# A 1024-by-256 matrix product inside a graph-network kernel, done with seven smaller products instead of eight

## The chip, the cores and the metric

The kernel runs on one core of a Trainium2 chip. The metric is the time of one execution on the device, in microseconds. The kernel before takes 3191.79 us, the median of three runs that lie between 3191.39 and 3193.04. The profile is of one more execution, whose span is 3188.7 us.

## What is computed

There are 64 graphs of 256 nodes with 256 features, and an integer adjacency matrix for each. Two layers follow one another. The first is two rounds of graph attention, then a norm, a feed-forward with ReLU, and a norm. The second is an attention with eight heads in which the adjacency value chooses which of several value matrices a pair of nodes uses, and then again a norm, a feed-forward with GELU, and a norm. Cut to the part that is changed:

```python
B, N, F = x.shape            # 64, 256, 256
# ... layer 0: two graph attentions, layernorm, relu feed-forward, layernorm
# ... layer 1: q, k, v, masked attention over 8 heads, output projection
x = _ln(src + attn_out, g1, beta1)
ff = jax.nn.gelu(x @ W1 + b1, approximate=False) @ W2 + b2     # W1: 256x1024, W2: 1024x256
return _ln(x + ff, g2, beta2)
```

Everything is in 32-bit floats. "The second product of the second feed-forward" is the multiplication by `W2`.

## The kernel before

Two graphs make a unit, so that there are 32 units of 512 rows. The program is a row of turns. In one turn three units are at work: `y_` in its second layer (attention, then the GELU feed-forward), `x_` in the ReLU feed-forward, and `z` in its two graph attentions. The order of TensorE and of the SyncE queue is that of the program text. VectorE (DVE), ScalarE (ACT) and GpSimd (POOL) are ordered by a scheduler; `behind(...)` keeps it from issuing an operation ahead of a marked one. There are six PSUM banks for general use (`bank`), besides one for `po` and one for `zo`.

```python
def turn(y_, x_, z):
    q, k_ = queries_keys(y_, hT)
    scores(0)                       # exponentials of the first quad of heads
    v = values(y_, hT, range(T))
    scores(1); piece(); sums(0)
    first_hidden(range(0, 2)); scores(2); sums(1)
    first_hidden(range(2, 5)); scores(3); piece()
    first_hidden(range(5, 8))
    # ... early(z), load_x(z + 1)
    sums(2); sums(3)
    out_(0); piece(); project(z); out_(1); first_rows(z)
    normed(y_, 2, y)
    # ... transposes of y_ by DVE and small DMAs; first_softmax(z); affine passes
    hidden_out(x_, 0, X["y"], X["h1"], wf2)
    for n, _ in enumerate(hidden_seven(y_, 1, hT, w1s, b1, AF.Gelu, h1)):
        if Z and n > 1:
            Z["hp"] = gat_first(z, Z["s"], Z["xp"], Z.get("hp"), range(2 * n - 4, 2 * n - 2))
    with behind("copied"):
        normed(x_, 1, X["y"])
    # ... transposes of x_, affine
    second_scores(z)                # rows by TensorE, then the softmax
    if waiting:
        finish(*waiting.pop(), 0, G)    # last norm of the unit of the turn before
    # ... (the last two turns differ)
    for t in range(T):
        if t == T - 1:
            second_sums(z)
        hidden_out_block(y_, 1, y, h1, w2, t)
    waiting.append((y_, y))
```

The first product of the GELU feed-forward already uses seven products for a two-by-two split (`hidden_seven`). The second product is done block by block, each of 128 rows, with 256 moving columns:

```python
def hidden_out_block(u, l, y, h1, wo_, t):
    b, i = divmod(t, NB)
    if i == 0:
        hidden_ps[u, l] = bank(f"yfp{l}_{u}_{b}")
    ps = hidden_ps[u, l]
    for k in range(FB):             # 8 blocks of the 1024 hidden features
        nc.tensor.matmul(ps[:, i * F:(i + 1) * F], h1[:, k, t * P:(t + 1) * P], wo_[:, k, :],
                         start=(k == 0), stop=(k == FB - 1))
    if i == NB - 1:
        yb = y[:, b * NB:(b + 1) * NB, :].rearrange("p t f -> p (t f)")
        nc.vector.tensor_tensor(yb, ps, yb, ALU.add)
```

The division of the attention ends with a check sum on ScalarE, and small vectors are brought in through a shared buffer of the tag `rz`:

```python
def divided(u, b, po, zo, oT):
    rz = work.tile([P, KB * N], F32, tag="rz", name=f"rz{u}_{b}")
    nc.vector.reciprocal(rz, zo)
    nc.vector.tensor_tensor(oT[:, :, b * N:(b + 1) * N], ...)
    nc.scalar.activation(rz, rz, AF.Identity, accum_out=low[:, u * G + b:u * G + b + 1])

def normed(u, l, y, blocks=range(T)):
    for t in blocks:
        nc.vector.bn_stats(...); nc.vector.bn_aggr(...)
    nc.gpsimd.tensor_scalar(rs, ...); nc.gpsimd.tensor_tensor(rs, rs, mhalf, ALU.pow)
    nc.vector.scalar_tensor_tensor(nm, ...)
    for t in blocks:
        nc.scalar.activation(y[:, t, :], y[:, t, :], AF.Identity, bias=nm[:, t:t + 1], scale=rs[:, t:t + 1])
```

Of the kernel before, what the change touches and what calls it, by code (L numbers as in the profile page):

```python
# [16 lines left out]
P = 128  # L17
# [368 lines left out]
def narrow_path(  # L386
# [97 lines left out]
    def columns(vs, name, queue):  # L484

        ns = [v.shape[0] // P for v in vs]
        rows = work.tile([P, KB * N], F32, tag="rz", name=f"{name}r")[:, 0:P]
        t = const.tile([P, sum(ns)], F32, name=name)
        at, views = 0, []
        for v, n in zip(vs, ns):  # L490
            queue.dma_start(rows[at:at + n, :], v.rearrange("(c p) -> c p", p=P))
            views.append(t[:, at:at + n])
            at += n
        ps = bank(f"{name}p")
        nc.tensor.transpose(ps[:, :at], rows[:at, :], ident[:at, :at])
        nc.vector.tensor_copy(t, ps[:, :at])
        return views
# [61 lines left out]
    def seven(w, name):  # L559
# [9 lines left out]
        return a11, a12, a22, s1, s2, a21, s4  # L569


    def shifted(w, blocks, shift, bias, name):
# [11 lines left out]

    w1s = []

    def folding():
# [19 lines left out]
        scaled(w1, lg3)  # L607
        w1s.extend(seven(w1, "w1"))
        yield

# [3 lines left out]
    for rb, v, name in ((rb1, g_bf2, "rbf2"), (rb2, t_bo, "rbo"), (rb3, t_b2, "rbt2")):  # L614
        nc.gpsimd.tensor_add(rb, rb, row(v, name, work.tile([P, KB * N], F32, tag="rz", name=name)[:, :F]))

# [10 lines left out]
    def to_features(src, name):  # L627

        dst = work.tile([P, KB, TN], F32, tag="hT", name=name)
        for k in range(KB):  # L630
            ps = bank(f"{name}p{k}")
            for t in range(T):
                nc.tensor.transpose(ps[:, t * P:(t + 1) * P], src[:, t, k * P:(k + 1) * P], ident)
            nc.vector.tensor_copy(dst[:, k, :], ps)
        return [dst[:, k] for k in range(KB)]
# [7 lines left out]
    def normed_features(u, l, xn, natural=False, queues=(nc.sync,)):  # L643
# [7 lines left out]
        if natural:  # L651
            hT = work.tile([P, KB, TN], F32, tag="hT", name=f"hT{u}_{l}")
            to = hT.rearrange("c k (t a r) -> c (k t) a r", a=Q, r=32)
            for q in range(Q):
                for a in range(Q):
                    nc.sync.dma_start(to[q * 32:(q + 1) * 32, :, a],
                                      yt[a * 32:(a + 1) * 32, q].rearrange("c k t r -> c (k t) r"))
            return [hT[:, k] for k in range(KB)]
# [82 lines left out]
    def add_blocks(u, name, y, b, lhs, rhs, n):  # L741
# [7 lines left out]
        yb = y[:, b * NB:(b + 1) * NB, :].rearrange("p t f -> p (t f)")  # L749
        nc.vector.tensor_tensor(yb, ps, yb, ALU.add)  # L750

# [38 lines left out]
    def hidden_seven(u, l, hT, w, bi, func, h1):  # L790
# [58 lines left out]
        for h in halves:  # L849
            product(two[h], h, s1, moving(0), True)  # L850
            p5[h] = copied(h, 1, two[h])
        for h in halves:
            product(two[h], h, s4, quarter[1][1], False)
            copied(h, 0, two[h])
# [8 lines left out]
        for h in halves:  # L863
            product(one[h], h, s3, moving(2), False)
            added(h, 1, 1, p5[h])
        yield
        for h in halves:
            product(one[h], h, a22, moving(3), False)
            done(h, 1, 0, one[h])
            done(h, 1, 1)  # L870

    def hidden_out_block(u, l, y, h1, wo_, t):
# [7 lines left out]
        if i == NB - 1:  # L880
            yb = y[:, b * NB:(b + 1) * NB, :].rearrange("p t f -> p (t f)")
            nc.vector.tensor_tensor(yb, ps, yb, ALU.add)

    hidden_ps = {}
# [32 lines left out]
    def weighted(u, b, m, q, k_, aT):  # L917
# [13 lines left out]
        for a in range(HPB):  # L931
            nc.scalar.activation(e[:, a, :], ps[a], AF.Exp, scale=isd)  # L932
        for a in range(0, HPB, 2):
            nc.vector.tensor_tensor(ea[:, a:a + 2, :], e[:, a:a + 2, :],  # L934
                                    ab[:, None, :].to_broadcast([P, 2, NB * N]), ALU.mult)
        es = work.tile([P, HPB, N], F32, tag="es", name=f"es{n}")
        nc.vector.tensor_add(es, e[:, :, 0:N], e[:, :, N:2 * N])
        return e, ea, es
# [14 lines left out]
    def divided(u, b, po, zo, oT):  # L953
        rz = work.tile([P, KB * N], F32, tag="rz", name=f"rz{u}_{b}")
        nc.vector.reciprocal(rz, zo)  # L955
        nc.vector.tensor_tensor(oT[:, :, b * N:(b + 1) * N],
                                po.rearrange("p (m n) -> p m n", m=KB),
                                rz.rearrange("p (m n) -> p m n", m=KB), ALU.mult)
        nc.scalar.activation(rz, rz, AF.Identity, accum_out=low[:, u * G + b:u * G + b + 1])

# [22 lines left out]
    def first_scores(z):  # L983
        first_rows(z)
        first_softmax(z)

    def second_scores(z):
        d = g[z]
        d["s"] = gat_softmax(z, 1, d["hp"], score_rows(z, 1, d["hp"], F), F + 1, F, d["aT"])

# [13 lines left out]

    def out_pieces(u, y, h1):

        for t in range(T):
            hidden_out_block(u, 1, y, h1, w2, t)
            b, i = divmod(t, NB)
            if i == NB - 1:  # L1010
                finish(u, y, b, 1)
            yield

    def finish(u, y, b, n):

        bt = slice(b * NB, (b + n) * NB)
        normed(u, 3, y, range(b * NB, (b + n) * NB))
        with behind("added"):
            affine(y[:, bt, :], rg4, rb4)
# [6 lines left out]
    def turn(y_, x_, z):  # L1026
# [11 lines left out]
        def sums(n):  # L1038
# [4 lines left out]
            if m == KB - 1:  # L1043
                divided(y_, b, *acc[b], oT)

        def first_hidden(blocks):
            if X:
                X["h1"] = hidden(x_, 0, X["hT"], wf1, bf1, AF.Relu, blocks, X.get("h1"))

        scores(0)  # L1050
# [7 lines left out]
        first_hidden(range(2, 5))  # L1058
        scores(3)
        piece()  # L1060
        first_hidden(range(5, 8))
        if Z:
            early(z)
        if z + 1 < NG:
            load_x(z + 1)
        sums(2)
        sums(3)

# [15 lines left out]
        if Z:  # L1084
            with behind("transposed", "placed"):
                first_softmax(z)
        if X:
            affine(X["y"], rg1, rb1)
# [11 lines left out]
        if X:  # L1100
            with behind("copied"):
                normed(x_, 1, X["y"])
            X["hT"] = (normed_features(x_, 1, X["y"], natural=True) if Z
                       else to_features(X["y"], f"h2T{x_}"))
            with behind("added"):
                affine(X["y"], rg2, rb2)
        if Z:
# [3 lines left out]
        if Z:  # L1111
            second_scores(z)
        if waiting:
            with behind("scaled" if Z else "copied"):
                finish(*waiting.pop(), 0, G)
        if y_ >= NG - 2:
            last = out_pieces(y_, y, h1)
            if X:
                left.append(last)
            else:  # L1120
                for _ in last:
                    pass
            return
        for t in range(T):
            if t == T - 1:
                second_sums(z)
            hidden_out_block(y_, 1, y, h1, w2, t)
        waiting.append((y_, y))
# [6 lines left out]
    with tc.manual_schedule(engines={mybir.EngineType.PE, mybir.EngineType.SP}):  # L1135
# [20 lines left out]
        normed(0, 1, g[0]["y"])  # L1156
        next(fold)
        second_sums(1)
        g[0]["hT"] = to_features(g[0]["y"], "h2T0")
        affine(g[0]["y"], rg2, rb2)  # L1160
        for u in range(NG):
            turn(u, u + 1, u + 2)
# [54 lines left out]
```

## Time and profile before

| | before |
|---|---|
| time, median of 3 | 3191.79 us |
| span of the profiled execution | 3188.7 us |
| TensorE matmuls busy | 3137.3 us |
| TensorE weight loads busy | 2178.4 us |
| VectorE busy | 2117.7 us |
| ScalarE busy | 1547.8 us |
| GpSimd busy | 412.1 us |
| DMA traffic over the span | 37 GB/s |

The page of a profile gives each engine's busy time, then the span in 40 slices, then the chain of work that ended last, then groups of instructions. The timeline lists an engine's instructions in order: the start in microseconds from the beginning of the span, the time from the first start to the last end, the engine, the line of the kernel, the operation, output and input by name, the shape, and how many like it follow each other. The end of a matmul is modelled and overlaps the start of the next, so that the cost of a group is best read from its start to the start of the next group. A line number may be that of a helper.

### The profile page before, as it was taken

Reading aid. Unit: us, or ns where it says so; the run is one execution under the profiler, and the core shown is the slowest. Engines: PE = TensorE matmul, PEld = TensorE weight load, DVE = VectorE, ACT = ScalarE, POOL = GpSimd, SP = SyncE. Lnnn points to the kernel's source line nnn. Section 1 sums busy time; section 2 is a strip of 40 time slices with the busy share of each in tenths; the row PEclk is TensorE's granted clock in tenths of the full one; section 3 lists DMA queues with packets and bytes.
Section 4 is the critical chain, followed back from the end, with each engine's and each line's share of the span. In section 5 each row is a group of like instructions: output and inputs, shape, how many; then the busy total and the mean of one; then the engine's idle time right before and its main releaser. Section 6 shows DMA issues by size and latency. Waiting matters only on the chain.

```text
span 3188.7 us, 46935 instructions
## 1 busy us (share of the span) xinstructions
PE 3137.3 (98%) x17584; PEld 2178.4 (68%) x17584; DVE 2117.7 (66%) x3870; ACT 1547.8 (49%) x3076; POOL 412.1 (13%) x633
## 2 busy tenths in 40 slices
PE   8899999999999999999999999999999999999997
PEld 5577766677766677666677666777666776667755
DVE  3566666666676666676666666666766666766655
ACT  4255544555544545545545445554445455455543
POOL 1111011011011111110110110110101111101100
PEclk9999999999999999999999999999999999999999
DMA  5011112121111121121211121211112111211000
GB/s 144 19 37 37 21 35 44 39 44 29 26 39 40 42 44 26 24 43 39 44 37 22 34 44 39 44 29 24 40 39 44 40 28 25 44 39 31 24 12 15
DMA packets 461160, 117.09 MB, mean 37 GB/s; under 512 B 397400, under 2 KB 460288, under 8 KB 460928
## 3 DMA queue, kind: packets, MB, share of 16 engines
q1 hardware_dynamic: 450592, 106.60, 15.4%
q10 hardware_dynamic: 9280, 6.39, 0.7%
q8 instruction: 141, 2.31, 0.3%
q0 software_dynamic: 1056, 1.05, 0.1%
q14 instruction: 91, 0.75, 0.1%
HBM read 57.04 MB, written 16.78 MB: 23 GB/s over the span
## 4 chain that ended last, share of the span: by engine, by line
PE 91%; DVE 4%; ACT 1%; POOL 1%; DMA 1%; ACTq 1%; issue 1%; SPq 0%; DVEq 0%; POOLq 0%
PE yfp L878 24%; PE h1p L785 14%; PE po L947 7%; PE vp L910 7%; PE h1a L820 6%; PE sp L926 4%; PE h1b L820 4%; PE qp L897 4%; PE yop L747 4%; PE kp L897 3%; PE hpp L736 3%; PE xpp L694 3%; PE ygp L747 3%; PE zo L950 2%; POOL rs L764 1%; DVE st L761 1%
## 5 line engine op out<-in xcount | busy, mean ns | idle before, releaser
L934 DVE TENSOR_TENSOR ea<-e,aT 128x1024 f32<-128x1024 f32 x256 | 302.2, 1222 | 285.1 <-ACT e L932 285.1
L768 ACT ACTIVATE y<-y,nm,rs 128x256 f32<-128x256 f32 x512 | 269.4, 591 | 420.2 <-DVE nm L765 420.2
L878 PE MATMUL yfp<-w,h 128*128 128x256 f32 x2048 | 452.9, 379 | 0.0
L785 PE MATMUL h1p<-hT,wf 128*128 128x512 f32 x992 | 450.6, 602 | 0.0
L878 PE MATMUL yfp<-wf,h 128*128 128x256 f32 x2048 | 448.5, 380 | 0.0
L878 PEld LDWEIGHTS yfp<-wf,h 128*128 128x128 f32 x2048 | 387.8, 191 | 52.2 <-issue 0.5
L878 PEld LDWEIGHTS yfp<-w,h 128*128 128x128 f32 x2048 | 386.6, 190 | 51.9 <-DVE v L912 0.3
L932 ACT ACTIVATE e<-sp 128x512 f32<-128x512 f32 x512 | 263.7, 603 | 224.4 <-PE sp L926 218.1
L785 PEld LDWEIGHTS h1p<-hT,wf 128*128 128x128 f32 x992 | 180.6, 189 | 228.7 <-issue 193.1
L648 DVE STREAM_TRANSPOSE yt<-y 128x256 f32<-128x256 f32 x368 | 151.7, 431 | 214.7 <-ACT y L768 201.0
L787 ACT ACTIVATE h<-h1p,cols 128x512 f32<-128x512 f32 x256 | 172.8, 692 | 239.0 <-PE h1p L785 239.0
L763 POOL TENSOR_SCALAR rs<-mv 128x4 f32<-128x4 f32 (+1 forms) x130 | 29.1, 232 | 1751.0 <-DVE mv L762 1743.8
L955 DVE RECIPROCAL rz<-zo 128x512 f32<-128x512 f32 x64 | 214.7, 3354 | 53.6 <-PE zo L950 53.6
L665 POOL COPY hT<-yt 32x256 f32<-32x256 f32 x248 | 215.8, 870 | 191.9 <-DVE yt L648 166.1
L775 DVE TENSOR_TENSOR y<-y,rg 128x1024 f32<-128x1024 f32 (+1 forms) x130 | 157.0, 1209 | 98.5 <-ACT y L768 94.2
L910 PE MATMUL vp<-wv,hT 128*128 128x512 f32 x480 | 214.0, 599 | 0.0
L761 DVE BATCH_NORM_STATS2 st<-y 128x6 f32<-128x256 f32 x512 | 195.3, 408 | 4.5
L826 ACT COPY cp<-h1b 128x512 f32<-128x512 f32 x192 | 111.1, 581 | 113.4 <-PE h1b L820 70.1
L910 PEld LDWEIGHTS vp<-wv,hT 128*128 128x128 f32 x480 | 88.7, 190 | 110.4 <-issue 103.2
L776 DVE TENSOR_TENSOR y<-y,rb 128x1024 f32<-128x1024 f32 (+1 forms) x130 | 161.2, 1242 | 3.2
L830 DVE TENSOR_TENSOR h<-h1a,cp 128x512 f32<-128x512 f32 x192 | 130.3, 682 | 45.7 <-PE h1a L820 45.6
L696 ACT COPY xp<-xpp 128x260 f32<-128x260 f32 x128 | 47.6, 373 | 232.6 <-PE xpp L694 232.5
(183 smaller groups left out, 4773.1 us busy)
## 6 DMA issues: line engine op xcount, KB each, us to landing
hT<-yt SPq DMA_DIRECT2D x1038, 32.0 KB, 1.9
y<-in_x_dram SPq DMA_DIRECT2D x32, 512.0 KB, 4.0
xq<-in_x_dram SPq DMA_DIRECT2D x240, 64.0 KB, 2.3
aq<-in_adj_dram SPq DMA_DIRECT2D x240, 64.0 KB, 2.4
out_dram<-y SPq DMA_DIRECT2D x30, 512.0 KB
hT<-yt ACTq DMA_DIRECT2D x186, 32.0 KB, 1.9
wf<-in_L_gnn_w_ff_dram SPq DMA_DIRECT2D x2, 1024.0 KB, 7.1
w<-in_L_gnn_W_dram SPq DMA_DIRECT2D x2, 1024.0 KB
```

Of the source, the lines that this page charges most:

```text
L665: nc.gpsimd.tensor_copy(to, at)
L747: nc.tensor.matmul(ps[:, i * F:(i + 1) * F], lhs(t, k), rhs(b, k), start=(k == 0), stop=(k == n - 1))
L761: nc.vector.bn_stats(st[:, t, :], y[:, t, :])
L768: mark["normed"] = nc.scalar.activation(y[:, t, :], y[:, t, :], AF.Identity, bias=nm[:, t:t + 1], scale=rs[:, t:t + 1])
L785: nc.tensor.matmul(ps, wi[:, k, f * P:(f + 1) * P], hT[k], start=(k == 0), stop=(k == KB - 1))
L820: nc.tensor.matmul(ps[:, i * N:(i + 1) * N], w_[:, f * P:(f + 1) * P], m, start=first and i == 0, stop=True, skip_group_check=True)
L878: nc.tensor.matmul(ps[:, i * F:(i + 1) * F], h1[:, k, t * P:(t + 1) * P], wo_[:, k, :], start=(k == 0), stop=(k == FB - 1))
L897: nc.tensor.matmul(ps, w[:, k, m * P:(m + 1) * P], hT[k], start=(k == 0), stop=(k == KB - 1))
L910: nc.tensor.matmul(ps, hT[k][:, t * P:(t + 1) * P], wvf[:, k, :], start=(k == 0), stop=(k == KB - 1))
L932: nc.scalar.activation(e[:, a, :], ps[a], AF.Exp, scale=isd)
L934: nc.vector.tensor_tensor(ea[:, a:a + 2, :], e[:, a:a + 2, :], ab[:, None, :].to_broadcast([P, 2, NB * N]), ALU.mult)
L947: nc.tensor.matmul(po[hp, m * N:(m + 1) * N], vs[:, hp], w[:, a, j * N:(j + 1) * N], start=(n == 0), stop=(n == len(terms) - 1))
```

## The change

The 512x1024 matrix of hidden values and the 1024x256 weights are each split in two by two. With sums of the quarters taken first, seven products of quarters give the result in place of eight. The sums of the weights are taken once, on GpSimd; those of the hidden values in each turn, on VectorE. The purpose is less work for TensorE. The rest of the change makes room for it: the last norm of a unit is moved into the next turn, behind the exponentials of the third quad; the check sum after a division is moved away from it; a few copies change engine; in the second transposition of `x_` four of sixteen small DMAs become copies on GpSimd; and the last part of the folding of weights at the start comes after the second norm.

```diff
-        rows = work.tile([P, KB * N], F32, tag="rz", name=f"{name}r")[:, 0:P]
+        rows = work.tile([P, KB * N], F32, tag="rz", name=f"{name}r", bufs=1)[:, 0:P]
...
+    def seven_out(w, name):
+        h = F // 2
+        b11, b12, b21, b22 = (w[:, k * FB // 2:(k + 1) * FB // 2, o * h:(o + 1) * h]
+                              for k in range(2) for o in range(2))
+        t1, t2, t4 = (const.tile([P, FB // 2, h], F32, name=f"{name}t{n}") for n in (1, 2, 4))
+        nc.gpsimd.tensor_tensor(t1, b12, b11, ALU.subtract)
+        nc.gpsimd.tensor_tensor(t2, b22, t1, ALU.subtract)
+        nc.gpsimd.tensor_tensor(t4, b21, t2, ALU.subtract)
+        nc.gpsimd.tensor_tensor(b12, b22, b12, ALU.subtract)
+        return b11, b21, b22, t1, t2, b12, t4
...
     def to_features(src, name):
-            nc.vector.tensor_copy(dst[:, k, :], ps)
+            nc.scalar.copy(dst[:, k, :], ps)
...
     def normed_features(..., natural=True):
-                    nc.sync.dma_start(to[q * 32:(q + 1) * 32, :, a], ...)
+                    move = nc.gpsimd.tensor_copy if q == a else nc.sync.dma_start
+                    move(to[q * 32:(q + 1) * 32, :, a], ...)
...
     def hidden_seven(...):
             product(one[h], h, s3, moving(2), False)
             added(h, 1, 1, p5[h])
+            done(h, 1, 1)
         yield
         for h in halves:
             product(one[h], h, a22, moving(3), False)
             done(h, 1, 0, one[h])
-            done(h, 1, 1)
...
+    def hidden_out_seven(u, l, y, h1, w, s1, s2, s3, s4):
+        b11, b21, b22, t1, t2, t3, t4 = w
+        K2, F2 = FB // 2, F // 2
+        a11, a12, a21, a22 = (h1[:, k * K2:(k + 1) * K2, b * N:(b + 1) * N]
+                              for b in range(2) for k in range(2))
+        nc.vector.tensor_tensor(s1, a21, a22, ALU.add)
+        nc.vector.tensor_tensor(s2, s1, a11, ALU.subtract)
+        nc.vector.tensor_tensor(s4, a12, s2, ALU.subtract)
+        mark["quarters"] = nc.vector.tensor_tensor(s3, a11, a21, ALU.subtract)
+
+        def product(ps, a, w_, first):
+            for i in range(NB):
+                for k in range(K2):
+                    nc.tensor.matmul(ps[:, i * F2:(i + 1) * F2], a[:, k, i * P:(i + 1) * P], w_[:, k, :],
+                                     start=first and i == 0 and k == 0, stop=True, ...)
+
+        def added(b, o, ps):
+            yq = y[:, b * NB:(b + 1) * NB, o * F2:(o + 1) * F2]
+            nc.vector.tensor_tensor(yq, ps[:, :F].rearrange("p (i f) -> p i f", i=NB), yq, ALU.add)
+
+        product(one, a11, b11, True);  added(0, 0, one);  yield
+        product(two, s1, t1, True);    added(1, 1, two);  yield
+        product(ps, a12, b21, True);   added(0, 0, ps);   yield
+        product(one, s2, t2, False);   added(0, 1, one);  yield
+        product(two, s4, b22, False);  added(0, 1, two);  yield
+        product(one, s3, t3, False);   added(1, 1, one);  yield
+        product(one, a22, t4, False);  added(1, 0, one);  yield
...
     def divided(u, b, po, zo, oT):
-        rz = work.tile([P, KB * N], F32, tag="rz", name=f"rz{u}_{b}")
+        rz = work.tile([P, KB * N], F32, tag="rz", name=f"rz{u}_{b}", bufs=1)
...
+        return rz
+
+    def noted(u, b, rz):
         nc.scalar.activation(rz, rz, AF.Identity, accum_out=low[:, u * G + b:u * G + b + 1])
...
     def turn(y_, x_, z):
         scores(3)
+        with behind("exp3"):
+            noted(y_, 0, acc[0])
         piece()
...
+        if waiting:
+            finish(*waiting.pop(), 0, G, ("summed1", "exp2"), ("divided0",))
         sums(2)
         sums(3)
...
             with behind("transposed", "placed"):
                 first_softmax(z)
+                noted(y_, 1, acc[1])
...
-            with behind("copied"):
+            with behind("fifth"):
                 normed(x_, 1, X["y"])
...
-            second_scores(z)
-        if waiting:
-            with behind("scaled" if Z else "copied"):
-                finish(*waiting.pop(), 0, G)
+            second_rows(z)
...
-        for t in range(T):
-            if t == T - 1:
+        for n, _ in enumerate(pieces):
+            if Z and n == 2:
+                second_softmax(z)
+            if Z and n == 5:
                 second_sums(z)
-            hidden_out_block(y_, 1, y, h1, w2, t)
...
         normed(0, 1, g[0]["y"])
-        next(fold)
         second_sums(1)
         g[0]["hT"] = to_features(g[0]["y"], "h2T0")
         affine(g[0]["y"], rg2, rb2)
+        next(fold)
```

The seven bodies of the products are put on one line each here, and the names of banks are left out. In the last two turns the seven products are cut at each `yield` into pieces, which fill places among the exponentials.

## The prediction
> **What bounds the kernel now.** I read the busy shares first, then the slices, the chain of waits, and one turn of the steady state in the timeline, engine by engine.
>
> ```profile
> PE 3137.3 (98%) x17584; PEld 2178.4 (68%) x17584; DVE 2117.7 (66%) x3870; ACT 1547.8 (49%) x3076; POOL 412.1 (13%) x633
> ...
> PEclk9999999999999999999999999999999999999999
> ...
> PE 91%; DVE 4%; ACT 1%; POOL 1%; DMA 1%; ACTq 1%; issue 1%; SPq 0%; DVEq 0%; POOLq 0%
> ```
>
> TensorE is busy 98% of the span at full clock and makes up 91% of the chain that ended last; DVE has a third of its time free. The kernel is a row of 32 turns, and one turn in the middle lasts 96.58 us (from the first `h1b` matmul at 1526.02 to the next at 1622.60). Adding up start-to-start times in that turn leaves about 1 us without matmul issue. So only TensorE time, or a new TensorE wait, can move the result by much. The part that is replaced stands in the timeline of TensorE so:
>
> ```profile
> 1541.87 0.60 PE L703 MATMUL rows<-ident,hp 128*128 128x128 f32 x4
> 1542.31 10.53 PE L878 MATMUL yfp<-w,h 128*128 128x256 f32 x48
> 1552.67 3.62 PE L747 MATMUL ygp<-hp,s 128*128 128x256 f32 x16
> 1556.13 3.62 PE L878 MATMUL yfp<-w,h 128*128 128x256 f32 x16
> 1559.58 3.60 PE L897 MATMUL qp<-hT,wq 128*128 128x512 f32 x8
> 1563.01 3.60 PE L897 MATMUL kp<-hT,wk 128*128 128x512 f32 x8
> ```
>
> Columns: start, length, engine, line, form, count. The second product takes 10.36 + 3.45 = 13.81 us of each turn, counted start to start. It has 32 matmuls in the program and 64 records: an f32 matmul appears as two records, each with its own weight load. One record costs 13.81 / 64 = 216 ns at 256 columns; at 512 columns, from `qp`, (1563.01 − 1559.58) / 8 = 429 ns. So a record costs about 3 ns + 0.832 ns per column, and at 128 columns I expect 109.5 ns from the moving side.
>
> [...] The new matmuls stream 128 columns for each load of 128 weight columns, a balance this kernel never had. [...] The start of the trace has the two halves apart:
>
> ```profile
> 22.96 1.04 PE L679 MATMUL aTp<-ident,first 128*128 128x128 f32 x8
> 23.83 1.04 PE L633 MATMUL xT1p<-ident,y 128*128 128x128 f32 x8
> ...
> 53.92 1.84 PE L576 MATMUL b1sp<-cols,w 128*128 128x1 f32 x16
> ```
>
> Eight transposes, each with a load and 128 moving columns, take 23.83 − 22.96 = 0.87 us: 109 ns each, agreeing with the line above. The `b1sp` matmuls move one column per load, so they show the load's pace: (1.84 − 0.25) / 15 = 106 ns[...]. (Their records show loads of 190 ns, but these overlap; a transpose's load is shown with 137 ns, so it is perhaps a lighter one, and the transposes don't prove the balanced case.) No run shows both sides full at once.
>
> **The change part by part.**
>
> *Product.* Out: 64 records × 216 ns = 13.81 us. In: seven products × 2 row blocks × 4 k-blocks = 56 matmuls = 112 records of 128 columns. Columns fall from 8192 to 7168, by an eighth. 112 × 109.5 ns = 12.26 us. Gain **1.55 us a turn**, if loads hide.
>
> *Sums on DVE.* Four sums of quarters of 128x1024 cost 1.22 us each (the `es` row of the same shape), 4.9 us; seven additions of 128x256 at about 0.42 us (as the `tt` subtractions of that size), 2.9 us; two additions of 0.66 us go. Net +6.5 us a turn, so DVE busy goes from 66 us to some 73 of 95 us: not the bound. The order matters: product 1 needs no sum and covers 1.75 us; the second needs the first sum, whose input (the quarter for the second graph's upper half) has its GELU moved forward. Walking the turn with the old durations, that GELU ends near 1541.5, the first sum near 1542.8, and product 2 starts near 1544; the last sum is done near 1546.5, seven to eight us before product 6 ends. `second_sums` needs the scaled `hp` near 1553.3 and gets it near 1552.6. Narrow, but free.
>
> *ScalarE order.* The `rows` transposes wait for the last two `hp` copies. Before, they ran just in time:
>
> ```profile
> 1541.44 0.37 ACT L738 COPY hp<-hpp 128x258 f32<-128x258 f32 x1
> 1541.69 0.52 ACT L837 ACTIVATE h<-h,cols 128x256 f32<-128x256 f32 x1
> ```
>
> Now all four GELUs of the moved quarter (0.41 us each) stand ahead of the last two of these copies on ScalarE, where before two GELUs stood ahead of the last one; a normalizing row and one check sum of 0.8 us move too. I place the last copy between 1541.9 and 1542.4, so a wait of 0 to 0.5 us: I charge **0.2 us a turn**.
>
> *Deferred norm.* `finish` moves from the dense stretch behind the second product to the third quad of the next turn. Its two affine passes (1.22 + 1.23 us) fall where DVE sat idle 2.34 us before `ea` at 1593.84, its statistics (about 2 us) in the 3.56 us idle before `ea` at 1584.01. Both gaps are nearly filled, no more. TensorE reads `ea` of the last quad some 3 us later. Worth about 0.
>
> *Diagonal pieces to GpSimd.* 4 of 16 small DMAs become copies of about 0.9 us on an engine busy 13%: hidden; `qp` needs them 10 us later. Worth 0.
>
> *Head.* The folding of the first weights moves behind the norm. Before, GpSimd scaled and combined weights from 92.02 to 100.48, the norm's power waited in between, and `qp` started at 107.58, 17.3 us after the first feed-forward's last matmul at 90.30. Redoing that chain without it (addition 0.7, statistics 1, GpSimd 1.3, norms 4, transposes and copies on ScalarE) I get about 10.5 us: −6.5 us. Against it, the vector rows now share one buffer, so the ten small `colsr` loads start behind the first transpose at 6.55 instead of at 2.34, and take 7 to 8 us: the transpose of them, at 14.26 before, slips to about 17.5: +3.5. Net **−3 us**. The four weight sums for seven products (1.27 us each on GpSimd) are hidden.
>
> *Tail.* Turn 30's product is cut in seven pieces instead of four, five of which lie among the exponentials of turn 31, where TensorE waited 2.75 and 2.79 us for DVE. **About −2 us**.
>
> Sum: 32 × (1.55 − 0.2) = 43; 43 + 3 + 2 = 48; 3191.8 − 48 = 3144, rounded up to 3145 since narrow places err to one side.
>
> **The rivals.**
>
> *Weight loads take over.* The pace at 128 columns is not 109.5 but what load and matmul take partly in line. At 123 ns, 112 records cost the old 13.8 us and the gain is gone (head and tail leave 3190 to 3195 with the waits)[...]. At 190 ns, the length of a load record, it would be 21.3 us a turn and 3430. For: PEld is 387 us busy on 2048 loads in the `yfp` row. Against: the 106 ns pace of `b1sp`, whose loads are recorded as 190 ns too.
>
> *A new wait ends the stage.* ScalarE or DVE orders leave TensorE waiting at `rows`, at products 2, 4 and 6 (bank held until DVE has added), or at `ygp`. One microsecond of it a turn eats 32 us and gives about 3170. For: DVE's four sums stand in one block ahead of the additions. Against: seven products of 1.75 us leave each addition a whole product of slack.
>
> *DVE becomes the bound.* 73 of 95 us says no, unless the exponential stage, where it already trails, slips: at most 1 us a turn.
>
> **Range and chances.** The full gain with no waits is 32 × 1.55 + 5 = 55, 3137; a larger head and tail could give 3125. On the other side, partly hidden loads with waits give 3170 to 3195. Range 3122 to 3192. The line for faster by over 2% is 3128: it needs every term at its best and some stalls of the old kernel removed besides, 0.12. Slower by over 2% (3256) needs 140 ns a record: 0.06. Within 2%: 0.82.
>
> **What would show it.** In the new timeline, x16 groups of 128x128 about 1.75 us apart would prove the pace; 2 us or more, the first rival. No more than 0.3 us between the last `h1a` and the next group ahead of `rows` proves the ScalarE charge. A turn of 95.2 us, `qp` of turn 0 near 104.5, DVE near 74% and TensorE still 98% would bear out the sum. A turn of 96.5 or more would make it wrong.

## Result and profile after

The changed kernel takes **3160.78 us** (median of 4 runs, 3155.64 to 3163.95) against 3192.41 us for the kernel before in the same runs (3191.39 to 3193.23): a ratio of **0.990, 95% interval 0.9882 to 0.9917**. That is 31.6 us less, where the prediction had 48 less. The busy shares and the granted clock of the page after:

```profile
PE 3097.2 (98%) x19120; PEld 2199.1 (70%) x19120; DVE 2329.8 (74%) x4146; ACT 1548.6 (49%) x3088; POOL 521.2 (17%) x757
...
PEclk8999999999999999999999999999999999999998
```

TensorE does 1536 more matmul records in 40 us less busy time, DVE is at 74% as forecast, and the first and last slices of the granted clock now show 8 in place of 9: it is 0.83 instead of 0.94 over the first 79 us, and 0.90 instead of 0.93 over the last. That is the outline of the whole case: the middle gained, in sum, what was forecast, and the ends lost some of it.

The names in the timelines of TensorE: `yf` is the second product done in seven parts and `yfp` a plain one, `h1a` and `h1b` the first product of the GELU feed-forward, `h1p` that of the ReLU one; `qp` and `kp` are queries and keys, `sp` the scores, `yop` the output projection; `ygp` are the sums of the second graph attention, `hp` the features that it sums, `rows` the transposed rows of its scores; `h2T` and `h3T` are transposed features.

The replaced product, in TensorE's timeline of a middle turn (start, length, engine, line, form, count; the last line is cut short by the end of the window that was read):

```profile
1624.11 0.60 PE L716 MATMUL rows<-ident,hp 128*128 128x128 f32 x4
1624.55 1.95 PE L913 MATMUL yf<-w,h 128*128 128x128 f32 x16
1626.33 1.95 PE L913 MATMUL yf<-w2t,eq 128*128 128x128 f32 x16
1628.12 1.95 PE L913 MATMUL yf<-w,h 128*128 128x128 f32 x16
...
1635.27 3.62 PE L760 MATMUL ygp<-hp,s 128*128 128x256 f32 x16
1638.72 1.95 PE L913 MATMUL yf<-w2t,h 128*128 128x128 f32 x16
1640.51 1.45 PE L959 MATMUL qp<-hT,wq 128*128 128x512 f32 x3
```

Groups of 16 stand 1.787 us apart, 111.7 ns a record. From the first group to `ygp`, and from the last group to `qp`, the product takes 10.72 + 1.79 = 12.51 us instead of 13.81. No wait stands ahead of `rows` or between the products.

I split the span at two starts, the first `qp` of turn 0 and of turn 31, read from the timelines:

| stretch (us) | before | after | difference | forecast |
|---|---|---|---|---|
| start to `qp` of turn 0 | 107.58 | 113.42 | +5.8 | −3 |
| turns 0 to 30 | 2987.29 | 2942.16 | −45.1 | −43 (for 32) |
| `qp` of turn 31 to the end | 93.8 | 102.0 | +8.2 | −2 |
| span | 3188.7 | 3157.6 | −31.1 | −48 |

### The profile page after: what moved, and what is told of

Its sections match the earlier page's. It is cut to its first block, busy times and chain, and to the rows that moved or that the text cites. A ratio compares the mean times of both kernels' runs of the same rounds, so it can differ in the third digit from the quotient of the medians.

```text
span 3157.6 us, 50461 instructions
## 1 busy us (share of the span) xinstructions
PE 3097.2 (98%) x19120; PEld 2199.1 (70%) x19120; DVE 2329.8 (74%) x4146; ACT 1548.6 (49%) x3088; POOL 521.2 (17%) x757
## 3 DMA queue, kind: packets, MB, share of 16 engines
q8 instruction: 153, 2.51, 0.3%
## 5 line engine op out<-in xcount | busy, mean ns | idle before, releaser
L996 DVE TENSOR_TENSOR ea<-e,aT 128x1024 f32<-128x1024 f32 x256 | 312.2, 1261 | 51.1 <-ACT e L994 47.0
L776 POOL TENSOR_SCALAR rs<-mv 128x4 f32<-128x4 f32 (+1 forms) x130 | 54.8, 421 | 1692.0 <-DVE mv L775 1686.4
L678 POOL COPY hT<-yt 32x256 f32<-32x256 f32 x248 | 241.2, 973 | 185.0 <-DVE yt L661 177.3
L661 DVE STREAM_TRANSPOSE yt<-y 128x256 f32<-128x256 f32 x368 | 162.6, 442 | 97.1 <-ACT y L781 88.6
L988 PEld LDWEIGHTS sp<-q,k 32*128 32x128 f32 x2048 | 92.7, 184 | 109.6 <-issue 72.8
L961 ACT ACTIVATE q<-qp,cols 128x512 f32<-128x512 f32 x64 | 43.3, 677 | 255.1 <-PE qp L959 255.1
L918 DVE TENSOR_TENSOR y<-yf,y 128x256 f32<-128x256 f32 x224 | 93.3, 417 | 84.8 <-PE yf L913 84.7
```

Source lines behind the costliest of these rows:

```text
L661: mark["transposed"] = nc.vector.transpose(yt[:, :, :, t].rearrange("p q k r -> p k q r"), xn[:, t].rearrange("p (k q c) -> p k q c", k=KB ...
L678: nc.gpsimd.tensor_copy(to, at)
```

## Experiments

My theory after the result: the product's gain is the 45 us of the turns in the table, about the 43 forecast, and head and tail (the first and the last row) lost 14 us through three orders that can be undone (the shared vector buffer, the weight sums on GpSimd, the pieces in the last turn). The rivals: the turns' 45 us are partly something else, and the product at 128 columns is worth less than it looks; or head and tail cost nothing by themselves.

### The old product with the rest of the change

All second products of the GELU feed-forward are plain again, in four pieces of 256 columns, and the weight sums on GpSimd go with the seven products; the other parts of the change stay, with the work between the pieces placed for four of them.

```diff
-        for n, _ in enumerate(hidden_out_seven(u, 1, y, h1, w2s, *s)):
-            if last and n in (4, 6):
+        for t in range(T):
+            hidden_out_block(u, 1, y, h1, w2, t)
+            if last and t % NB == NB - 1:
```

> The changed kernel with the old second product in every turn (32 matmuls of 256 columns, two additions, no sums of quarters); the moved norm, check sums, copies and folding stay. Theory, the product is nearly the whole gain: a steady turn takes 96.3 to 96.6 us against 95.30, every turn alike, so that the moved norm is worth only the 0.2 us a turn by which the mean turn before (96.80) exceeded its shortest (96.58); total about 3195 to 3200 with the slower start and end. Rival, the rescheduling brought the gain: a turn below 95.8 us and a total below 3180.

Measured: 3189.63 us (20 runs, 3186.16 to 3192.10), ratio to before 0.9986 [0.9979, 0.9993]. The split of its span is the instructive part: 111.78 us of head, 2973.45 us of turns, 104.9 us of tail. Against the kernel before, the rest of the change took 13.8 us off the turns (2987.29 to 2973.45) and put 4.2 on the head and 11.0 on the tail. That tail is longer than the changed kernel's, without any seven products: four pieces stand in the new places, each two of them followed by a norm on DVE, and the second `yop` waits for the quotient.

```profile
3139.53 3.75 PE L759 MATMUL yop<-wo,q 128*128 128x256 f32 x8 [6.94 <-DVE q L1017]
```

Of the 13.8 us, 11.1 lie in turns 1 to 29 and 3.1 in turn 30; turn 0 is 0.4 longer. Against the changed kernel, the seven products took **31.3 us** off the turns (2973.45 to 2942.16): a middle turn is 96.36 us with the old product and 95.30 with the new one, 1.06 us, not 1.35. So the 45 us that seemed to confirm the forecast were 31 for the product and 14 for things that I had given nothing.

### The deferred norm put back

The last norm of a unit runs again beside the second product of the next one.

```diff
-        if waiting:
-            finish(*waiting.pop(), 0, G, ("summed1", "exp2"), ("divided0",))
...
             if Z and n == 2:
                 second_softmax(z)
+                if waiting:
+                    finish(*waiting.pop(), 0, G, ("scaled",), ("scaled",))
```

> The changed kernel with the last norm of a unit put back to where it was, beside the second product of the next unit, behind the scaling of hp. Theory, seven products leave DVE too little room there: the two affine passes of 2.45 us and the statistics of 2 us push the additions back, products 6 and 7 or ygp wait for DVE, a turn takes 95.6 to 97 us instead of 95.30, total 3170 or more. Rival, DVE has enough slack there too, as at 74% busy: a turn stays within 0.1 us of 95.30 and the total within 3 us of 3161.

Measured: 3173.12 us (3168.36 to 3174.61), 0.9939 [0.9924, 0.9955]: 12.3 us slower than the changed kernel. Its turns 0 to 30 take 2955.55 us, 13.4 more, and a middle turn 95.73. The waits of TensorE from 100 to 3060 us (who waited, for whom, us in total, times, longest), first with the norm back, then of the changed kernel:

```profile
PE sp L988 <- ACT k L961: 10.5, 30, 0.4
...
PE h1a L833 <- DVE h L843: 1.3, 3, 0.5
```

```profile
PE sp L988 <- ACT k L961: 5.1, 30, 0.2
```

With the norm back, the scores wait twice as long for the key copies, since the norm's passes on DVE and ScalarE push the next norm's rows later (4.12 us behind `qp` instead of 3.93); and the first `h1a` group on weight sums takes 1.95 us to the next group instead of 1.73. That makes 0.19 + 0.22 = 0.41 of the 0.43 us between the two turns. The kernel before has the same 1.94 us at that group (1.73 in the version with the old product), and it waits there besides, in 8 turns and for up to 0.84 us (waits from 100 to 3100 us):

```profile
PE h1a L820 <- DVE h L830: 4.6, 8, 0.8
```

The changed kernel has none of these waits; with the norm back three return. In turns 1 to 29 putting the norm back costs 14.8 us (2779.5 against 2764.7), more than the 11.1 that the rest of the change gained there with the old product: the longer wait of the scores, 0.19 us a turn, comes only beside the seven products. So the deferral is enough to account for what these turns gained beyond the product, though the norm was not put back alone beside the old product. The 3.1 us of turn 30 are something else: 1.7 of them are `yop` and the group behind it, which ran longer in the kernel before after a wait of 2.79 us for DVE, and 1.5 a wait for a norm on ScalarE.

### Pace: half the streamed columns

Each matmul of the second product streams 64 of its 128 columns; the other half of that product is left out of the output.

```diff
-  nc.tensor.matmul(ps[:, i * F2:(i + 1) * F2], a[:, k, i * P:(i + 1) * P], w_[:, k, :],
+  nc.tensor.matmul(ps[:, i * F2:i * F2 + 64], a[:, k, i * P:(i + 1) * P], w_[:, k, :64],
```

> The changed kernel with every matmul of the seven products cut to 64 of its 128 columns, and the additions too; half of the second product is left out, so that the output lacks it. Theory, the weight load sets the pace at 128 columns or is just level with it: records follow each other every 106 to 108 ns, a group of 16 in about 1.71 us, and a turn is at most 0.6 us shorter. Rival, load and matmul stand partly in line: 111.7 minus about 53, so near 60 ns, a group of 16 in about 0.95 us, and a turn some 5.9 us shorter.

Measured: 3312.02 us in one run, 151 us more with half the streaming. The timeline of a middle turn says two things:

```profile
1699.17 1.95 PE L913 MATMUL yf<-w2t,eq 128*128 128x64 f32 x16
1700.96 1.95 PE L913 MATMUL yf<-w,h 128*128 128x64 f32 x16
...
1710.78 5.41 PE L760 MATMUL ygp<-hp,s 128*128 128x256 f32 x16 [2.51 <-ACT hp L739]
```

First, the pace is unchanged: 1700.96 − 1699.17 is 1.79 us at 64 columns as at 128. The streaming side was not the limit. (The first and the last of the groups, next to other forms, take 1.73.) Second, the longer time has another cause. The shorter DVE additions led to another instruction order, in which the fourth to sixth addition stand ahead of the softmax products on DVE. The scaled `hp` comes late, `ygp` waits 2.51 us, and then takes 5.24 us to the next group instead of 3.45. The granted clock in windows of that turn (window, its length, busy time of PE, PEld, DVE, ACT and POOL, clock, DMA share, GB/s) is lower there:

```profile
1700.00:1708.00 8.00, 8.00 (x75) 8.00 (x73) 3.80 (x9) 2.26 (x3) 0.00 (x0) 1.00 0.45 71
1711.00:1717.00 6.00, 6.00 (x26) 5.03 (x25) 2.44 (x7) 0.92 (x3) 0.00 (x0) 0.72 0.00 0
```

Over 6 us behind the 2.51 us without work the clock is 0.72 on average; it is 1.00 again from 1718 to 1725. The wait and the longer `ygp` make 2.51 + 1.79 = 4.3 us, which is what the turn grew by (95.30 to 99.58). As a time this run says nothing on the product; as a timeline it settles which side did not limit it.

### Pace: half the loaded columns

The other side alone: each load brings 64 weight columns, 128 are streamed, and the DVE additions keep their length, so that the order stays. Half of the rows of that product are left out of the output.

```diff
-  nc.tensor.matmul(ps[:, i * F2:(i + 1) * F2], a[:, k, i * P:(i + 1) * P], w_[:, k, :],
+  nc.tensor.matmul(ps[:64, i * F2:(i + 1) * F2], a[:, k, i * P:i * P + 64], w_[:, k, :],
```

> Every matmul of the second product loads 64 weight columns instead of 128 and still streams 128; half of the output rows of that product are left out, the DVE additions keep their length. In the run with 64 streamed columns per 128 loaded ones the groups of 16 records stood 1.787 us apart, as in the changed kernel with 128 streamed ones. If the weight load sets the pace of the balanced stream, halving it uncovers the streaming side: groups of 16 records 1.75 us apart (109.5 ns a record, the rate worked out in the prediction from the 256- and 512-column rows). If instead the 111.7 ns are the streaming side plus a fixed cost for each pair, the groups stay at 1.787 us. The turn would be 0.24 us shorter in the first case (7 x 0.035), unchanged in the second. No time is read from a single run.

```profile
1626.41 1.91 PE L913 MATMUL yf<-w2t,eq 128*64 128x128 f32 x16
1628.15 1.91 PE L913 MATMUL yf<-w,h 128*64 128x128 f32 x16
```

Groups are 1.745 us apart, 109.1 ns a record: the streaming pace of the prediction. So in the changed kernel the **weight load** sets the pace, at 111.7 ns, just above the 109 ns of the stream, and the two overlap: nothing close to their sum is seen. The turn itself is 95.47 us, not shorter, because the groups next to a change of width (`rows` to `yf`, `yf` to `ygp` and back, `yf` to `qp`) are 0.1 to 0.2 us longer here; the expected turn was missed, the expected distance of groups was met.

### The head: a buffer of its own for the vector rows

```diff
-  rows = work.tile([P, KB * N], F32, tag="rz", name=f"{name}r", bufs=1)[:, 0:P]
+  if name == "cols":
+      rows = work.tile([P, KB, TN], F32, tag="q", name=f"{name}r", bufs=1)[:, 0, 0:P]
+  else: (as before)
```

> The changed kernel, but the ten small vectors at the start go into a buffer of their own. Theory, the shared buffer: the wait of 8.27 us ahead of the colsp transpose vanishes, colsp runs near 14.3 us instead of 22.82, qp of turn 0 starts some 8 us earlier (near 105), and the total falls from 3160.8 to about 3152; steady turns stay at 95.30. Rival, the queue of large loads at the start sets the pace and the buffer only rearranges it: colsp comes earlier, but qp of turn 0 moves by less than 3 us. If the weight sums on GpSimd then fall beside other DVE work, up to 4 us of the gain may be lost.

Measured: 3153.83 us (3149.30 to 3154.96), 0.9872 [0.9855, 0.9888], 7.0 us less than the changed kernel. There, the transpose of the rows waits for the loads (last column: us idle, and what ended it; the releaser named is the load of `wo`, while in the version with the plain last product a wait of 8.77 us at the same place is put down to the last of the ten loads):

```profile
22.82 0.28 PE L495 MATMUL colsp<-ident,colsr 32*128 32x32 f32 x1 [8.27 <-DMA wo<-in_L_gnn_Wo_dram]
```

With its own buffer the same transpose starts at 14.49 and `qp` at 106.57 instead of 113.42. The shared buffer cost 8.6 us at the transpose against the kernel before, not 3.5: the ten loads are issued from 7.06 to 20.57 instead of from 2.34 to 9.67, so they start later and are also further apart.

### The head: weight sums behind the first feed-forward's

```diff
+        with behind("folded1", "folded2"):
-        w2s.extend(seven_out(w2, "w2"))
+            w2s.extend(seven_out(w2, "w2"))
```

> The changed kernel, but the four sums of the second weights on GpSimd are held back until the sums of the first weights are done. Theory, GpSimd slows DVE [...]: the masked products s<-s,aT between 35 and 41 us fall from up to 1.49 us to 0.42 us, the wait of 3.45 us ahead of rows goes, qp of turn 0 starts about 4 us earlier, total about 3157. Rival, the late wv load on DVE or the cold clock is the cause: the wait ahead of rows stays at 3 us or more and the total stays at 3161.

Measured: 3155.74 us (3155.18 to 3157.28), 0.9883 [0.9867, 0.9900], 5.0 us less. In the changed kernel the four sums fall among the softmax products of the head (timelines of DVE and GpSimd):

```profile
34.71 0.42 DVE L733 SCALAR_TENSOR_TENSOR s<-s,aT 128x256 f32<-128x256 f32 x1
...
35.05 1.49 DVE L733 SCALAR_TENSOR_TENSOR s<-s,aT 128x256 f32<-128x256 f32 x1
```

```profile
34.83 1.44 POOL L577 TENSOR_TENSOR w2t<-w 128x512 f32<-128x512 f32 x1 [31.21 <-DMA w<-in_L_gnn_W_dram]
```

The same DVE instruction takes 0.42 us before GpSimd begins and 1.49 beside it; it ends at 36.54, 0.27 us after GpSimd's sum at 36.27. In all, four DVE products that take 0.42, 0.69, 0.42 and 0.42 us with the sums moved take 1.49, 1.75, 0.66 and 1.47 beside them, 3.4 us more, and the reciprocal of that softmax starts at 41.07 against 37.23. Why they take longer beside GpSimd is not shown. `rows` then waits 3.45 us for `xp`, and 0.36 in the version with late sums. How much of it is hit differs with the moment at which the weights land: in the six other versions with the same head, `ygp` stood at 56.7 to 57.2 (four) and at 60.7 and 62.1, in the changed kernel at 61.7, with late sums at 56.3. The runs of the changed kernel lie within 8.3 us, those with late sums within 2.1. One thing keeps me from booking all 5 us here: the version with the old product has no such sums and `ygp` at 56.7, and still `qp` at 111.78 against 108.59, because its matmuls from `ygp` on took longer: `ygp` 6.21 us to the next group, where the changed kernel has 3.45 at a granted clock of 1.00, and 14.4 us from there to `h1p` instead of 12.4. In the six versions with the same head `qp` stood between 108.65 and 115.67, so a head read from one profile is uncertain by several us, and the +5.8 of the table is one reading; the middle one of the seven is 110.9, or +3.3.

### The tail: piece order, and a plain last product

First, the third piece of the next-to-last unit's product goes behind the scores of the fourth quad.

```diff
-            else:
+            elif blocks.start != 2:
                 piece()
...
             noted(y_, 0, acc[0])
         piece()
+        if not X:
+            piece()
```

> The changed kernel, but in the last turn the third piece of the product of turn 30 stands behind the fourth quad's scores instead of ahead of them. Theory, the piece holds a bank that the scores need, and its addition stands behind the reciprocal on DVE: the wait of 3.37 us ahead of sp goes, the exponentials of the fourth quad start about 4 to 5 us earlier counted from qp of turn 31, and the total falls by 3 to 5 us to about 3156. Rival, DVE's own work is what the last turn runs on: the wait only moves to the next po or yop, and the total stays within 1 us.

Measured: 3160.10 us (3157.72 to 3163.83), 0.9899 [0.9882, 0.9915]: no gain. What it repairs is visible in the changed kernel, where the scores of the fourth quad wait for an addition that is queued on DVE behind a reciprocal (TensorE, then DVE):

```profile
3089.25 1.13 PE L988 MATMUL sp<-q,k 32*128 32x256 f32 x10 [3.37 <-DVE y L918]
```

```profile
3085.56 3.35 DVE L1017 RECIPROCAL rz<-zo 128x512 f32<-128x512 f32 x1
3088.83 0.36 DVE L918 TENSOR_TENSOR y<-yf,y 128x256 f32<-128x256 f32 x1
```

That wait is gone with the new order, and the last scores are done 28.8 us after `qp` instead of 34.8. But the second `yop` then waits 4.72 us instead of 1.86 for the quotient `q`, and the tail stays at 101.8 us against 102.0.

Second, the last unit's product is plain, with 256 columns; GpSimd restores the quarter of the weights that had been overwritten.

```diff
+        if u == NG - 1:
+            nc.gpsimd.tensor_tensor(b12, b22, b12, ALU.subtract)
+            for t in range(T):
+                hidden_out_block(u, 1, y, h1, w2, t)
```

> The changed kernel, but the last unit's second product is done plainly, in 32 matmuls of 256 columns (GpSimd first restores the one quarter of the weights that was overwritten). Theory, at the end nothing hides the sums and additions of the seven products: from the first yf of the last unit to the end of the product takes 13.9 us instead of 16.4, and the total falls by about 2.5 us to 3158. Rival, the cold TensorE clock made it long: the plain product is as long as before relative to its 13.8 us and the total doesn't change.

Measured: 3159.74 us (3157.39 to 3161.64), 0.9895 [0.9879, 0.9912]. The intervals overlap the changed kernel's; the timeline shows the effect: the last product takes 13.98 us without a wait instead of 16.4 with two (1.74 us for the first sum of quarters, 1.47 for an addition), and the tail is 100.0 instead of 102.0. Here, where nothing lies beside it, the seven products with their sums are slower than the plain one.

### All four together, and the norm that swallowed the piece order

> The changed kernel with the four repairs together: own buffer for the vectors, weight sums held back, piece moved, last product plain. If they add up (8 + 4 + 4 + 2.5), about 3142 us; if the head's two share their gain (the buffer moves the sums away from the DVE work anyway), about 3146.

Measured: 3144.16 us (3141.61 to 3148.43), 0.9845 [0.9831, 0.9858], with `qp` of turn 0 at 103.29 and a tail of 99.8. In this tail DVE adds up three pieces at 3083.90 and then runs the norm of the next-to-last unit's first row block before its second reciprocal at 3090.09. So one more order was tried: that norm behind the second quotient.

```diff
-            if last and n in (4, 6):
-                finish(u, y, n // 6, 1)
+            if last and n in (5, 6):
+                finish(u, y, n - 5, 1, ("divided1",))
```

> As the version with own buffer, late sums, piece order and plain last product, and the norm of the next-to-last unit's first row block issued behind the second quotient. In that version the third piece behind the fourth scores started the last exponentials 6 us earlier, but the tail was no shorter: DVE ran that norm (3083.90 to 3090.09) ahead of its second reciprocal of 3.35 us, and the second yop waited 4.73 us instead of 1.86. If this order is what swallowed the gain, the second reciprocal starts some 3.8 us earlier (right behind the third addition, as soon as zo is done near 3086.3), the wait of yop is near 1 us, and the tail from qp to the end falls from 99.8 to 96 to 97 us: 3141 against 3144. Rival: the norm's work lands in front of the last unit's own norm instead, h3T starts no earlier, and the time stays at 3144.

Measured: **3141.16 us** (3140.60 to 3147.99), **0.9838 [0.9825, 0.9852]**. The wait of the second `yop`, first with all four, then with the norm moved:

```profile
3094.73 3.63 PE L764 MATMUL yop<-wo,q 128*128 128x256 f32 x8 [4.73 <-DVE q L1022]
```

```profile
3087.15 1.97 PE L764 MATMUL yop<-wo,q 128*128 128x256 f32 x8 [1.07 <-DVE q L1022]
```

The tail falls from 99.8 to 96.1 us, as expected. The piece order had helped; a norm on DVE had taken its gain. The intervals of these two versions overlap, so that the last 3 us rest on the timelines.

### The norm behind the key copies

The wait of 0.17 us for the key copies in each turn (0.24 us from `qp` to the scores: 7.20 us, 6.96 with the old product) has its cause on ScalarE:

```profile
1547.13 0.69 ACT L961 ACTIVATE q<-qp,cols 128x512 f32<-128x512 f32 x1 [8.24 <-PE qp L959]
1549.14 2.08 ACT L781 ACTIVATE y<-y,nm,rs 128x256 f32<-128x256 f32 x4 [1.32 <-DVE nm L778]
1551.12 0.66 ACT L961 ACTIVATE q<-qp,cols 128x512 f32<-128x512 f32 x1
1551.69 1.28 ACT L961 ACTIVATE k<-kp,cols 128x512 f32<-128x512 f32 x2
```

Four rows of the norm stand between the first and the second copy, and the copies behind them come late. Two versions issue that norm behind the four copies: the changed kernel with it, and the version with own buffer, late sums and plain last product with it.

```diff
+        q, k_ = queries_keys(y_, hT)
+        if X and x_ > 1:
+            normed(x_, 0, X["y"], then=("keyed",))
+            X["hT"] = normed_features(x_, 0, X["y"])
```

> The norm that follows the graph sums of the next-but-one unit is issued on ScalarE behind the four copies of queries and keys instead of between the first and the second. My reading: in the changed kernel qp to the first scores takes 7.20 us a turn, with the old product 6.96, because only one product of 1.79 us instead of 3.45 us is left between ygp and qp, so that the four normalizing rows (2.08 us) fall in among the copies and the last key copy ends late. Then this order gives 6.96 again, the wait of sp for k goes, turns are 95.06 us, and the time falls by 30 x 0.24 = 7 us, to about 3153. Rival: the wait only moves: the exponentials of the first quad stand behind the rows now, 2 us later, and the first po matmuls wait for them; or h1p waits for the features: the turn then stays at 95.3 or grows, 3160 or more.

> Own buffer for the vector rows, second weight sums behind the first, the last unit's product plain, and the norm behind the key copies; the order of the pieces in the last turn is left as it was, since moving it gave a later wait of 4.7 us in place of 1.9. If the gains add: the version without the norm's move and with the piece order took 3144; less 7 us for the norm: 3137. If the norm's move only shifts a wait: 3144 to 3150.

Measured: 3201.43 us (8 runs, 3199.16 to 3208.14), 1.0031 [1.0020, 1.0042], and 3191.64 us (12 runs), 0.9995 [0.9986, 1.0004]. The first is 40.7 us slower than the changed kernel, and the second misses the expected 3137 by 55. The reading of the wait was right, from `qp` to the scores it is 6.97 us again, but the rival held:

```profile
1575.89 0.70 PE L989 MATMUL sp<-q,k 32*128 32x256 f32 x4
1576.90 1.72 PE L989 MATMUL sp<-q,k 32*128 32x256 f32 x12 [0.31 <-DVE v L975]
```

The second quad's scores, 1.08 us before, last 2.67 us. The rows start 7.66 us behind `qp` instead of 3.93, behind them DVE's transposes of the norm, then its masked products, then its `v` copies, and the scores need a bank that these copies empty. The turn is 96.65 us, 1.35 more: the small wait had been the cheapest place for a delay that must stand somewhere.

## Why the prediction was right and where it was wrong

The time lies in the range and within 2% of the kernel before, which was given 0.82; the sum was 16 us off, and several terms were wrong in ways that partly cancel.

- **Pace.** Forecast 109.5 ns a record, measured 111.7. That loads would hide was my assumption; no run before had shown it. The first rival was true in its mildest form: loads set the pace, but hidden, and the 123 ns that would have used up the gain did not come. The `b1sp` row that I used for the load (106 ns with one streamed column) was 5 ns low for loads beside full streams; why, was not tried. It costs 112 × 2.2 ns = 0.25 us a turn.
- **Waits.** I charged 0.2 us at `rows`, behind the GELUs. There is none. 0.24 us a turn stand at the scores instead. I had walked the old turn up to `ygp` only; with 1.79 us of product left between `ygp` and `qp` instead of 3.45, the norm behind `ygp` meets the query and key copies. So the product's term is 1.55 − 0.25 − 0.24 = 1.06 us, just what the two versions' turns differ by: 31 us in all, not 43.
- **Deferred norm.** "Worth about 0" was wrong: putting it back costs 12.3 us. I had asked whether its new place was free, and it was; I had not asked whether its old place was on the path. The waits of up to 0.84 us at `h1a`, in 8 turns of the kernel before, were there to be read in its view of waits.
- **Turns in sum.** 95.2 us forecast, 95.30 measured, but as 1.06 + 0.22 below the shortest turn before, helped by the lost waits of its longer turns. A right sum of wrong terms, by luck.
- **Head.** −3 forecast, +5.8 measured in one profile (108.65 to 115.67 for `qp` with the same head, where 104.5 was forecast). The fold's chain from `ygp` to `qp` is 10.6 us as forecast (10.5). The shared buffer cost 8.6 us at the transpose where I had 3.5, and the weight sums on GpSimd, "hidden", held up DVE.
- **Tail.** −2 forecast, +8.2 measured. I had two waits of 2.75 and 2.79 us to fill in turn 31, but the second one, at 3059.76, lies in turn 30, where it stays (2.86). And I counted the pieces as filling and not what they queue on DVE, their additions and the norm behind them: three pieces instead of one ahead of the last scores, the wait of 3.37 us behind a reciprocal, two more waits in the last product. The seven products alone are not the cause: with the old product in the same places, and its norms among them, the tail is 104.9. A further part is matmuls at a lower clock: the `h1` stage of the last unit starts after idle stretches of 2.35 and 1.51 us, and its first three groups take 1.86, 1.71 and 1.71 us at a granted clock of 0.50, where they took 0.97, 0.86 and 0.87 at 1.00.
- **DVE.** 74% and not the bound in the turns: as forecast. In the tail it ended four of TensorE's waits (3.37, 1.86, 1.74 and 1.47 us).

The range held because the errors (31 + 14 in place of 43, and +14 in place of −5) left 31 us of gain; it is not that each step was known. Of the tail 2.3 us against the kernel before remain even in the best version (96.1 against 93.8), and their cause was not looked for.

## What to carry to other kernels

Price a moved operation at both ends, what its new place hides and what its old place was holding up; and after shortening a stage, walk on into the next one, since work that used to finish under the removed time now meets its first instructions. Keep head and tail as sums of their own: an order that is free in a full pipeline is not free where nothing runs beside it, and there the plain form can be the faster one. Before removing a small steady wait, ask where the delay goes: here 0.24 us became 1.6.

## What the hardware showed that was not expected

- In f32, pairs of one load and one matmul at 128 columns run at 111.7 ns with 128 or 64 streamed columns, and at 109.1 with 64 loaded ones. That fits the larger of the two sides, with nothing left unhidden; that a load beside one streamed column takes 106 stays unexplained.
- In the run with half the streamed columns, `ygp` took 5.24 us to the next group behind an idle stretch of 2.51 us, instead of 3.45, and the granted clock from 1711 to 1717 us was 0.72; over the whole run it was 0.965, in the changed kernel 0.991.
- The length of such a stretch alone does not decide. In turn 30 the second `yop` waits 2.86 us in the changed kernel and in four other versions: half the loaded columns, the norm behind the key copies (two versions), and the norm behind the quotient. In the changed kernel it then takes 3.48 us to the next group, at a granted clock of 0.51, and in the first version with the norm behind the key copies 3.36; in the other three it takes 1.80. The norm behind the key copies, then half the loaded columns:

```profile
3062.23 3.52 PE L760 MATMUL yop<-wo,q 128*128 128x256 f32 x8 [2.86 <-DVE q L1019]
```

```profile
3024.23 1.97 PE L760 MATMUL yop<-wo,q 128*128 128x256 f32 x8 [2.86 <-DVE q L1018]
```

  So 1.7 us of the changed kernel's turn 30 come and go with no cause that these profiles show. What decides was not tried.
- A DVE product of 128x256 (`s<-s,aT`) went from 0.42 to 1.49 us beside a GpSimd sum of 128x512. That sum took 1.44 us, where the four sums of that size in the kernel before took 1.26 to 1.27.
